# A four-layer sequence model on one core: the end of a channel mix beside the next layer norm, and key products whose sums grow in PSUM

## The chip, the cores and the metric

One NeuronCore of a Trainium2 chip runs the whole kernel in one launch. The metric is the device time of that launch in microseconds (us). TensorE (PE) does the matrix products; VectorE (DVE), ScalarE (ACT) and GpSimd (POOL) do the rest; the DMAs stand in the queue of SyncE (SP), which issues them in order.

## The reference

The input x is 8 sequences of 112 tokens with 512 channels, and there is a context of 8 x 375 x 512; everything is float32. Four layers follow each other: a small cross attention, two RWKV layers (time mix, then channel mix), and a last layer of two cross attentions with 16 heads of 128 channels and an MLP. What the change touches is the end of the second channel mix and the last layer:

```python
rr = jax.nn.sigmoid(xr2 @ fWr.T)
kk = jnp.square(jax.nn.relu(xk2 @ fWk.T))
x = x1 + rr * (kk @ fWv.T)
...
h = layer_norm(x, ln1_scale, ln1_offset)
q, k, v = h @ wq + bq, ctx @ wk + bk, ctx @ wv + bv
k, v = concat([k, bias_k]), concat([v, bias_v])
x = x + softmax(q @ k.T / sqrt(128)) @ v @ wo + bo
# the same with ln2, wq2, ..., then the MLP
x = x + gelu(layer_norm(x) @ w_fc1 + b_fc1) @ w_fc2 + b_fc2
```

## The kernel before, in words

Activations lie with their channels on the 128 partitions, in four chunks (NC = 4), and the 896 tokens in the free dimension, in two halves of 448 (NH). x stays in SBUF for the whole kernel. A projection (`project`, L152) makes, for each half h and output chunk o, one PSUM bank from four matmuls and gives it to an evacuation function.

**The order of the work.** The program is written as one stream for all engines. A framework keeps the engines' instructions in an order that it derives from that stream and from estimated costs (only the time mix, L632, has its order fixed by hand), and puts in the waits. Tiles come from pools; a tile of a pool with a few buffers waits until the last reader of the tile in the same buffer is done, and a pool that is opened after another was closed reuses its memory, so its tiles wait for the old ones there. `fill(n)` pulls n pieces of work from a generator named `filler`, which puts independent matmuls at that place of the stream: while the RWKV layers run it is `values()`, which makes the values of both cross attentions (and a few keys) ahead of time and stores them in DRAM; before each attention it is `first_keys()`.

**The second channel mix** (`channel_mix`, L674) norms x, mixes, and does three projections fk, fr, fv. fv's evacuation (`add`) multiplies the bank by rr on DVE (L722) and adds it to x on POOL (L723).

**The layer norm** (`layer_norm_half`, L165) works on one half of the tokens at a time: DVE sums the four channel chunks (L174, L176), one matmul with a matrix of 1/512 makes the mean for every channel (L178), DVE subtracts (L183), ACT squares (L185), DVE and PE make the variance in the same way, ACT takes the root (L190, Sqrt needs a table load), DVE the reciprocal (L191) and the product (L192), and ACT multiplies with the scale and adds the offset of each chunk (L194). Between the steps, `fill` puts matmuls.

**A cross attention** (`attention`, L1050; twice, i = 1, 2) norms x into h_in, and works in four groups gr of four heads. For each group it makes queries of all tokens, then goes through the eight sequences b: scores (L1167), softmax (L205 to L212), four transposes of the probabilities (L1170), their copies (L1174, L1176), the product with the values (L1180), the sum with a bias (L1187). Keys are made for two sequences b, b + 1 at a time. After a group comes its part of the output projection, which adds to x.

**Seven products instead of eight.** Queries, keys, output projections and MLP use a scheme of the Strassen kind: `seven` (L970) has a matrix product cut into 2 x 2 blocks made from seven block products, of sums of blocks of the weight (`weight_sums`, four POOL instructions, L957 to L960) and sums of blocks of the other operand (`token_sums`, four DVE instructions, L965 to L968; for keys the sums of the context lie in DRAM, and are loaded as four tiles cs of 375 KB, beside cx and cy, the plain context, by `key_pieces`, L1060). A block product is two matmul calls of the program, and shows as four instructions on PE. It is done for two halves m of the output chunks, so a pair of sequences and a group take 14 block products. In `seven`, each m uses the banks of the tag mm, of which there are two: the first product is copied out as p1 by ACT (L1001); the sums u2 = p + p1 (L1011) and u3 = p + u2 (L1016) are made by DVE as it reads the banks, and DVE adds them again to the later banks as it writes the keys (L1088); one product per m goes straight to the keys by an ACT copy (L1086). That is 4 ACT copies and 10 DVE additions from PSUM for a pair.

**Around the norms.** `attention` opens with `filler = first_keys()`, which loads the group's key weight, makes its POOL sums and yields the 14 products of the first pair; fill(3), then the norm with fills of 2, 2, 4 and 2, 2, 2, then the token sums, the queries and the loop over the sequences, which takes what is left of the filler. POOL also copies one column of bias into each key tile (L1160).

**The pools of layer 3** (`layer3`) are opened in this order: t3v (key sums with two buffers, the cs tiles, u2 and u3), t3k (cx, cy, three key tiles, values), t3 (h_in, q, t_h and others), t3w, and the PSUM pools.

Of the kernel before, what the change touches and what calls it, by code (L numbers as in the profile page):

```python
# [22 lines left out]
F32 = mybir.dt.float32  # L23
# [6 lines left out]
P = 128  # L30
B, L, C, S = 8, 112, 512, 375
N = B * L
# [9 lines left out]
HG = 4  # L42
# [66 lines left out]
def tile_kernel(ctx: ExitStack, tc: tile.TileContext, d: dict, out: bass.AP):  # L109
# [39 lines left out]
    def mm(ps, name):  # L149
        return ps.tile([P, 512], F32, tag="mm", name=name)  # L150

    def project(ps, w, rhs, evacuate, name, hs=(0, 1)):  # L152

        for h in hs:
            for o in range(NC):
                p = mm(ps, f"ps_{name}_{o}_{h}")[:, :NH]
                for k in range(NC):
                    nc.tensor.matmul(
                        p, w[:, k, o * P : (o + 1) * P], rhs(k, h), start=k == 0, stop=k == NC - 1
                    )  # L160
                evacuate(o, h, p)

    def layer_norm_half(ps, work, y, h, scale, offset, name, room=None, bank=None, fills=(2, 2, 4)):

        def small(tag, what):
            if room is not None:
                return room[1][:, h, int(tag == "rstd")]
            return work.tile([P, NH], F32, tag="rstd", name=f"{tag}_{what}_{name}_{h}")  # L170

        def over_channels(z, what):
            part = small("part", what)
            nc.vector.tensor_add(part, z[:, 0], z[:, 1])  # L174
            for c in range(2, NC):
                nc.vector.tensor_add(part, part, z[:, c])  # L176
            p = bank(f"{what}_{name}_{h}") if bank else mm(ps, f"{what}_{name}_{h}")[:, :NH]
            nc.tensor.matmul(p, mean_c, part, start=True, stop=True)  # L178
            return p

        mean = over_channels(halves(x, h), "mean")
        fill(fills[0])
        nc.vector.tensor_sub(y, halves(x, h), mean.unsqueeze(1).to_broadcast([P, NC, NH]))  # L183
        sq = work.tile([P, NC, NH], F32, tag="half", name=f"sq_{name}_{h}") if room is None else room[0][h]
        nc.scalar.activation(sq, y, AF.Square)  # L185
        fill(fills[1])
        var = over_channels(sq, "var")
        fill(fills[2])
        rstd = small("rstd", "")
        nc.scalar.activation(rstd, var, AF.Sqrt, bias=eps)  # L190
        nc.vector.reciprocal(rstd, rstd)  # L191
        nc.vector.tensor_mul(y, y, rstd.unsqueeze(1).to_broadcast([P, NC, NH]))  # L192
        for c in range(NC):
            nc.scalar.activation(  # L194
                y[:, c, :], y[:, c, :], AF.Identity, bias=column(offset, c), scale=column(scale, c)
            )

    def layer_norm(ps, work, dst, scale, offset, name, room=None, bank=None):
# [473 lines left out]
            project(ps, w_o, lambda c, h: halves(y[:, c, :], h), add, f"o{n}")  # L672

    def channel_mix(n, pre, names, first):  # L674
        with (
            tc.tile_pool(name=f"c{n}", bufs=1) as one,
            tc.tile_pool(name=f"cw{n}", bufs=2) as work,
# [44 lines left out]
                nc.vector.tensor_mul(y, p, y)  # L722
                nc.gpsimd.tensor_add(xs, xs, y)  # L723

            project(ps, f_v, lambda c, h: halves(kk[:, c, :], h), add, f"fv{n}")

    def rwkv_layers():
        with tc.tile_pool(name="rc", bufs=1) as one:
# [219 lines left out]
    def weight_sums(pool, tag, w, u):  # L948


        if tag == "wv":
            y = pool.tile([P, NC, C], F32, tag=tag, name=f"ws{u}")
            y = [y[:, j].rearrange("p (k o) -> p k o", k=2) for j in range(4)]
        else:
            y = [pool.tile([P, 2, 256], F32, tag=f"{tag}{j}", name=f"ws{j}{u}", bufs=1) for j in range(4)]
        a11, a12, a21, a22 = (w[:, k : k + 2, o : o + 256] for o in (0, 256) for k in (0, 2))
        nc.gpsimd.tensor_add(y[0], a21, a22)  # L957
        nc.gpsimd.tensor_sub(y[1], y[0], a11)
        nc.gpsimd.tensor_sub(y[2], a11, a21)
        nc.gpsimd.tensor_sub(y[3], a12, y[1])  # L960
        return y
# [8 lines left out]
    def seven(ps, work, w, s, b, t, n, put, u):  # L970
# [35 lines left out]
        for m in range(2):  # L1006
# [18 lines left out]
            yield  # L1025
            put(1, m, q, u2)

    def quarters(y):

        return [halves(y[:, k : k + 2], h) for h in range(2) for k in (0, 2)]  # L1030
# [16 lines left out]

        return put

    def attention(i, h_in, work, kv, ps, ps2, keep, mlp_norm):  # L1050
        nonlocal filler
        pre = "L3_xattn_"
        scale = 1.0 / math.sqrt(HD)
# [6 lines left out]
        def key_pieces(gr, b, w, kts):  # L1060


            u = f"{i}_{gr}_{b}"
            if ("wk", i, gr, b) in shared:
                for j in range(2):
                    kts.append(kv.tile([P, HG, T], F32, tag="kt", name=f"k{u}_{j}", bufs=3))
                    for t in range(3):
                        y = shared["wk", i, gr, b + j][:, t]
                        nc.sync.dma_start(kts[-1][:, :, t * CT : (t + 1) * CT], y)
                return  # L1070
            cx = kv.tile([P, NC, S], F32, tag="cx", name=f"cx{u}", bufs=2)
            nc.sync.dma_start(cx, d["ctxT"][:, b])
            t = [shared["pool"].tile([P, 3, 2, CT], F32, tag="cs", name=f"cs{u}_{j}", bufs=4) for j in range(4)]
            for y, pos in zip(t, (BLOCKS + 1, 2, 4, 6)):
                at = (3 * (b // 2) * BLOCKS + pos) * BLOCK
                from_ = shared["blocks"][:, at : at + 3 * BLOCKS * BLOCK].rearrange("p (c n) -> p c n", c=3)
                nc.sync.dma_start(y.rearrange("p c k s -> p c (k s)"), from_[:, :, :BLOCK])
            b22 = kv.tile([P, 2, S], F32, tag="cx2", name=f"cy{u}", bufs=1)
            nc.sync.dma_start(b22, d["ctxT"][:, b + 1, 2:])
            kt = [kv.tile([P, HG, T], F32, tag="kt", name=f"k{u}_{j}", bufs=3) for j in range(2)]  # L1080
            kts += kt

            def put(j, o, p, y):
                dst = kt[j][:, o, :S]
                if y is None:
                    nc.scalar.copy(dst, p)  # L1086
                else:
                    nc.vector.tensor_add(dst, p, y)  # L1088

            t = [y.rearrange("p c k s -> p k c s") for y in t]  # L1090
            yield from seven(ps, work, *w, (cx[:, :2], cx[:, 2:], b22), t, S, put, f"k{u}")

        kts, w_ks = [], []

        def first_keys():
            w_ks.append(key_weight(0))
            yield from key_pieces(0, 0, w_ks[0], kts)

        def ln_bank(name):
            return ps2.tile([P, HG, L], F32, tag="av", name=name).rearrange("p a b -> p (a b)")  # L1100


        scaled = keep.tile([P, 2 * NC + HEADS], F32, tag="scaled", name=f"scaled{i}")
        for at, n, v in ((0, NC, f"ln{i}_scale"), (NC, NC, f"ln{i}_offset"), (2 * NC, HEADS, f"bq{i}")):
            nc.scalar.mul(scaled[:, at : at + n], vecs[:, _COL[pre + v] : _COL[pre + v] + n], scale)
        over = keep.tile([P, HEADS], F32, tag="over", name=f"over_k{i}")
        bias_k, bk = (vecs[:, _COL[pre + v] : _COL[pre + v] + HEADS] for v in (f"bias_k{i}", f"bk{i}"))
        nc.vector.tensor_sub(over, bias_k, bk)
        filler = first_keys()
        room = keep.tile([P, NC, N], F32, tag="q", name=f"room{i}")  # L1110
        t_h = keep.tile([P, 3, 2, NH], F32, tag="t_h", name=f"t_h{i}")
        fill(3)
        layer_norm(ps, work, h_in, scaled[:, :NC], scaled[:, NC : 2 * NC], f"ln3_{i}", ([halves(room, h) for h in range(2)], t_h), ln_bank)
        token_sums(nc.vector, *quarters(h_in), t_h)

        rows = kv.tile([HEADS, HD], F32, tag="rows", name=f"bvr{i}", bufs=1)
# [5 lines left out]
        def queries(gr):  # L1122

            w = weight(f"{pre}wq{i}", gr)
            q = keep.tile([P, HG, N], F32, tag="q", name=f"q{i}_{gr}")

            def put_q(h, o, p, y):
                bias, dst = column(scaled, 2 * NC + gr * HG + o), halves(q[:, o, :], h)
# [13 lines left out]
        for gr in range(NG):  # L1142
# [6 lines left out]
            for b in range(B):  # L1149
                u = f"{i}_{gr}_{b}"  # L1150
                tok = slice(b * L, (b + 1) * L)
                if b % 2 == 0:
                    if gr and not b:
                        w_ks.append(key_weight(gr))
                    for _ in filler if gr == b == 0 else key_pieces(gr, b, w_ks[gr], kts):
                        pass
                    if not b and not ends:
                        s_o = weight_sums(keep, "ws", w_o, f"o{i}_{gr}")
                kt = kts.pop(0)
# [54 lines left out]
                for _ in out_pieces:  # L1214
                    pass

    def mlp(h_in, work, ps, keep, t_h):
        pre = "L3_xattn_"


        def hidden(gr):


            w = weight(f"{pre}w_fc1", gr)
            hid = keep.tile([P, NC, N], F32, tag="q" if gr % 2 else "ctxt", name=f"hid_{gr}")

            def put(h, o, p, y):
                bias, dst = vec(f"{pre}b_fc1", gr * NC + o), halves(hid[:, o, :], h)
# [42 lines left out]

    def layer3():
        with (
            tc.tile_pool(name="t3v", bufs=2) as shared["pool"],
            tc.tile_pool(name="t3k", bufs=2) as kv,
            tc.tile_pool(name="t3", bufs=1) as keep,
            tc.tile_pool(name="t3w", bufs=2) as work,
            tc.tile_pool(name="t3p", bufs=2, space=PSUM) as ps,
        ):
            h_in = keep.tile([P, NC, N], F32, name="h_in")  # L1280
            with tc.tile_pool(name="t3s", bufs=1, space=PSUM) as ps2:
                def mlp_norm(h, bank):
                    if not h:
                        room = keep.tile([P, 3, 2, NH], F32, tag="t_h", name="t_mlp")
                        shared["t_mlp"] = room
                        squares = halves(h_in, 1)
                    else:
                        squares = halves(keep.tile([P, NC, N], F32, tag="q", name="room_mlp"), 1)
                    pre = "L3_xattn_ln_mlp_"
                    room = [None, squares] if h else [squares, None]  # L1290
                    room = room, shared["t_mlp"]
# [2 lines left out]
                    )  # L1294

                for i in (1, 2):
                    attention(i, h_in, work, kv, ps, ps2, keep, mlp_norm)
            mlp(h_in, work, ps, keep, shared["t_mlp"])

    shared["spill"] = ctx.enter_context(tc.tile_pool(name="spill", bufs=1, space=bass.MemoryType.DRAM))  # L1300
    shared["blocks"] = shared["spill"].tile([P, (UNITS + 3) * BLOCKS * BLOCK], F32, name="blocks")
# [83 lines left out]
```

## Time and profile before

| what | value |
|---|---|
| median of 3 runs | 3063.15 us (3061.47 to 3063.49) |
| the profiled execution | 3068.96 us |
| its span, from the first instruction to the last | 3067.1 us |
| PE busy | 2936.8 us, 96% |
| DVE, ACT, POOL busy | 55%, 27%, 25% |
| mean granted clock of PE | 0.978 |
| DMA | 401.59 MB, 131 GB/s on average |

Durations in the text are from the profiled execution; instants are microseconds from the start of its span. The last projection of the second channel mix runs from about 1506 to 1530, the first attention from there to about 2188, the second from there to about 2850, and the MLP to the end. In a row of the profile, `a<-b,c` means that the instruction writes a and reads b and c, by the names of the tiles in the program; x before a number is the count; a bracket at the end gives the idle time of the engine before the instruction and what it is thought to have waited for. "PE" rows are matmuls, "PEld" rows their weight loads, which overlap.

### The profile page before, as it was taken

Reading aid. Unit: us, or ns where it says so; the run is one execution under the profiler, and the core shown is the slowest. Engines: PE = TensorE matmul, PEld = TensorE weight load, DVE = VectorE, ACT = ScalarE, POOL = GpSimd, SP = SyncE. Lnnn points to the kernel's source line nnn. Section 1 sums busy time; section 2 is a strip of 40 time slices with the busy share of each in tenths; the row PEclk is TensorE's granted clock in tenths of the full one; section 3 lists DMA queues with packets and bytes.
Section 4 is the critical chain, followed back from the end, with each engine's and each line's share of the span. In section 5 each row is a group of like instructions: output and inputs, shape, how many; then the busy total and the mean of one; then the engine's idle time right before and its main releaser. Section 6 shows DMA issues by size and latency. Waiting matters only on the chain.

```text
span 3067.1 us, 29702 instructions
## 1 busy us (share of the span) xinstructions
PE 2936.8 (96%) x10130; PEld 1585.1 (52%) x10130; DVE 1698.1 (55%) x2556; ACT 834.5 (27%) x1730; POOL 767.3 (25%) x668
## 2 busy tenths in 40 slices
PE   8989999998999999989989999999999999999999
PEld 4734433333434433337446666656566665656544
DVE  1433279876133289865165555655756454645555
ACT  2122145442232144532132222212222121212311
POOL 2232246642232257542210202020001101010030
PEclk9989999999999999999989999999999999999999
DMA  7322288963112299854234353424333343423110
GB/s 253 131 76 71 74 237 250 272 185 110 66 54 70 79 267 266 259 151 146 71 99 147 112 158 102 151 84 142 108 100 115 119 146 100 146 92 101 48 55 24
DMA packets 192054, 401.59 MB, mean 131 GB/s; under 512 B 26856, under 2 KB 112392, under 8 KB 185120
## 3 DMA queue, kind: packets, MB, share of 16 engines
q1 hardware_dynamic: 191904, 399.70, 42.0%
q8 instruction: 81, 1.33, 0.2%
q14 instruction: 69, 0.57, 0.1%
HBM read 321.85 MB, written 77.91 MB: 130 GB/s over the span
## 4 chain that ended last, share of the span: by engine, by line
PE 49%; DVE 2%; ACT 1%; issue 0%; POOL 0%; ACTq 0%; DVEq 0%; POOLq 0%
PE av L1180 6%; PE sc L1167 5%; PE ps_k1k L983 5%; PE ps_k7k L983 5%; PE ps_k5k L983 5%; PE pt L1170 3%; PE ps_k6k L983 2%; PE ps_k7q L983 2%; PE ps_k5q L983 2%; PE ps_k1q L983 1%; PE ps_k5o L983 1%; PE ps_k7o L983 1%; PE ps_k5fc L983 1%; PE ps_k7fc L983 1%; PE ps_k1o L983 1%; PE ps_k6q L983 1%
## 5 line engine op out<-in xcount | busy, mean ns | idle before, releaser
L839 PE MATMUL ps_vk<-wv,cv 128*128 128x512 f32 x1336 | 619.2, 611 | 52.4 <-DVE k L864 15.6
L839 PEld LDWEIGHTS ps_vk<-wv,cv 128*128 128x128 f32 x1336 | 251.5, 194 | 401.1 <-issue 303.0
L210 ACT ACTIVATE prob<-sc,top 112x376 f32<-112x376 f32 (+1 forms) x264 | 151.8, 575 | 709.6 <-DVE top L207 588.3
L649 POOL TENSOR_TENSOR rs<-st,r 128x896 f32<-128x896 f32 x128 | 246.7, 1928 | 226.7 <-DVE st L645 189.9
L645 DVE TENSOR_TENSOR_SCAN st<-decay,kv 128x904 f32<-128x904 f32 x128 | 260.4, 2035 | 15.6 <-DMA cv<-blocks 3.4
L1167 PE MATMUL sc<-k,q 128*112 128x376 f32 x512 | 200.6, 484 | 1.0 <-ACT prob L210 0.8
L1180 PEld LDWEIGHTS av<-pts,v 125*128 125x128 f32 (+1 forms) x1536 | 183.2, 191 | 30.0 <-DVE pts L1176 15.1
L1180 PE MATMUL av<-pts,v 125*128 125x112 f32 (+1 forms) x1536 | 186.6, 275 | 1.0 <-DVE pts L1176 1.0
L1160 POOL COPY k<-over_k 128x4 f32<-128x4 f32 x64 | 15.8, 253 | 678.3 <-PE sc L1167 610.0
L983 PE MATMUL ps_k1k<-cx,w_L_xattn_wk 128*128 128x375 f32 x480 | 177.1, 481 | 2.3 <-ACT rstdk L1001 2.3
L207 DVE TENSOR_REDUCE top<-sc 112x1 f32<-112x376 f32 (+1 forms) x264 | 143.6, 545 | 29.3 <-PE sc L1167 14.7
L641 DVE TENSOR_TENSOR kv<-vp,k 128x904 f32<-128x904 f32 x128 | 140.9, 1101 | 32.0 <-ACT vp L543 26.1
L922 ACT COPY k<-ps_vk 128x512 f32<-128x512 f32 (+1 forms) x153 | 89.0, 582 | 170.8 <-PE ps_vk L839 161.3
L1170 PEld LDWEIGHTS pt<-ident,prob 112*125 112x125 f32 (+1 forms) x768 | 97.6, 175 | 61.5 <-DVE prob L212 36.0
L212 DVE TENSOR_SCALAR prob<-prob,total 112x376 f32<-112x376 f32 (+1 forms) x264 | 120.7, 460 | 7.1
L983 PEld LDWEIGHTS ps_k1k<-cx,w_L_xattn_wk 128*128 128x128 f32 x480 | 89.3, 191 | 60.1 <-issue 3.2
L1170 PE MATMUL pt<-ident,prob 112*125 112x112 f32 (+1 forms) x768 | 116.3, 273 | 2.9 <-DVE prob L212 2.8
L543 ACT COPY vp<-vj 128x896 f32<-128x896 f32 x124 | 112.8, 910 | 11.6 <-DMA vj<-rows 7.6
L1187 DVE TENSOR_TENSOR ctxt<-av,bv 128x448 f32<-128x448 f32 x64 | 40.0, 624 | 126.6 <-PE av L1180 126.6
L933 POOL TENSOR_TENSOR k<-k,k 128x512 f32<-128x512 f32 (+1 forms) x51 | 67.4, 1322 | 133.6 <-ACT k L932 110.2
L1167 PEld LDWEIGHTS sc<-k,q 128*112 128x112 f32 x512 | 78.8, 176 | 41.1 <-ACT prob L210 6.1
L983 PE MATMUL ps_k7k<-cs,wsk 128*128 128x375 f32 x240 | 88.5, 480 | 0.6 <-DVE k L1088 0.6
(372 smaller groups left out, 4719.6 us busy)
## 6 DMA issues: line engine op xcount, KB each, us to landing
vj<-rows SPq DMA_DIRECT2D x124, 448.0 KB
cv<-blocks SPq DMA_DIRECT2D x181, 251.5 KB
cs<-blocks SPq DMA_DIRECT2D x120, 375.0 KB
wvs<-k SPq DMA_DIRECT2D x128, 256.0 KB
v<-wvs SPq DMA_DIRECT2D x64, 512.0 KB
cx<-in_ctxT SPq DMA_DIRECT2D x38, 750.0 KB
v<-wvs SPq DMA_DIRECT2D x64, 252.0 KB
wvs<-k SPq DMA_DIRECT2D x64, 224.0 KB
```

The lines of the kernel that those rows point to most:

```text
L207: nc.vector.tensor_reduce(top, scores, AX.X, ALU.max, negate=True)
L210: nc.scalar.activation(prob, scores, AF.Exp, bias=top, accum_out=total)
L212: nc.vector.tensor_scalar(prob, prob, total, None, ALU.mult)
L543: nc.scalar.copy(vp[:, :, 1:], by_batch(vjs.pop((c, j))))
L641: nc.vector.tensor_mul(flat(kv), flat(vp), flat(k[:, c]))
L645: nc.vector.tensor_tensor_scan(flat(st), flat(decay[:, c]), flat(kv), 0.0, ALU.mult, ALU.add)
L649: nc.gpsimd.tensor_mul(by_batch(rs), st[:, :, :L], by_batch(r[:, c, :]))
L839: nc.tensor.matmul(to, left, right, start=start and n == 0, stop=k == 1, skip_group_check=True)
L983: nc.tensor.matmul(to, lhsT, rhs, start=start and k == 0, stop=k == 1, skip_group_check=not start)
L1167: nc.tensor.matmul(sc, q[:, o, tok], kt[:, o, :], start=True, stop=True)
L1170: nc.tensor.transpose(pt[t][:nt, o, :], prob[:, t0 : t0 + nt], ident[:L, :L])
L1180: nc.tensor.matmul(av[:, o, :], v[:nt, t, o * HD : (o + 1) * HD], pts[:nt, t, o, :], start=t == 0, stop=t == 2,)
```

## The change

It has five parts.

1. The fv projection of the second channel mix is cut into pieces (`values_pieces`). The first half of the tokens is done as before. The second half becomes the filler of the norm of the first half: that half's norm of layer 3 is computed inside `channel_mix`, into two tiles of the weights' pool (y and sq), without the scale; one piece is pulled ahead of it and one at each of its three fill places. `attention` later applies scale and offset from y into h_in (`scale_by_channel`).
2. A new pool, near, is opened ahead of the other pools of layer 3, and so lies where the pool of the values was. It holds h_in, q (and the norm's room), t_h, scaled, over and the context tiles cx.
3. `first_keys` makes the keys of two pairs (sequences 0, 1 and 2, 3) instead of one. The fills around the norms become 2 and 3, 3, 4 for each half, with fill(8) after them; the loop over the sequences stops pulling once the pair that it needs is made.
4. The keys use `chained` in place of `seven`: the same block products with the same operands in another order, in two banks per m. One bank grows through four of them (k1, then + k6, then + k7, and at the end + t3's), and is copied out after each; the other takes the rest. So u2 and u3 are copies of a bank that grows on. For a pair this makes 10 ACT copies, 4 DVE additions that read PSUM and 2 DVE additions in SBUF; in the first group's first two pairs ("busy") it makes 14 ACT copies and 6 POOL additions in SBUF.
5. The POOL sums of a key weight have one buffer instead of two; the key tiles have four instead of three.

Cut to its core:

```diff
+            def values_pieces(h):
+                for o in range(NC):
+                    project(ps, f_v, lambda c, h: halves(kk[:, c, :], h), add, f"fv{n}", [h], [o])
+                    yield
...
+                for _ in values_pieces(0):
+                    pass
+                filler = values_pieces(1)
+                fill(1)
+                y, sq = (
+                    wpool.tile([P, NC, C], F32, tag="w", name=f"{what}_ln3")[:, :, :NH] for what in ("y", "sq")
+                )
+                layer_norm_half(ps, work, y, 0, None, None, "ln3_1", ([sq], None), None, (1, 1, 1))
+                for _ in filler:
+                    pass
+                shared["normed"] = y
...
+    def chained(ps, work, w, s, b, t, n, dst, u, busy):
...
+        for m in range(2):
+
+            one, two = (mm(ps, f"ps_{what}{u}_{m}")[:, :n] for what in (("k1", "k5") if m == 0 else ("k5", "k1")))
+            grows, other = (one, two) if m == 0 else (two, one)
+            p1, u2, u3 = (tile_of(what, m) for what in ("p1", "u2", "u3"))
+            for p, left, right, start, to, add in (
+                (grows, lambda k: w[:, k], b11, True, p1, None),
+                (other, lambda k: s()[0][:, k], t[0], True, dst(1, 2 + m), None),
+                (grows, lambda k: s()[1][:, k], t[1], False, u2, None),
+                (other, lambda k: s()[3][:, k], b22, False, dst(1, m), u2),
+                (grows, lambda k: s()[2][:, k], t[2], False, u3, None),
+                (other, lambda k: w[:, 2 + k], b21, True, dst(0, m), p1),
+                (grows, lambda k: w[:, 2 + k, 256:], t[3], False, dst(0, 2 + m), None),
+            ):
...
+                yield
+                if add is None or busy:
+                    nc.scalar.copy(to, p)
+                    if add is not None:
+                        nc.gpsimd.tensor_add(to, to, add)
+                else:
+                    nc.vector.tensor_add(to, p, add)
+                if to is u3:
+                    (nc.gpsimd if busy else nc.vector).tensor_add(dst(1, 2 + m), dst(1, 2 + m), u3)
...
-            yield from seven(ps, work, *w, (cx[:, :2], cx[:, 2:], b22), t, S, put, f"k{u}")
+            yield from chained(
+                ps, work, *w, (cx[:, :2], cx[:, 2:], b22), t, S, lambda j, o: kt[j][:, o, :S], f"k{u}", gr == 0 and b < BH
+            )
...
         def first_keys():
+
             w_ks.append(key_weight(0))
-            yield from key_pieces(0, 0, w_ks[0], kts)
+            for b in (0, 2):
+                yield from key_pieces(0, b, w_ks[0], kts)
+                made.append(b)
...
-        fill(3)
-        layer_norm(ps, work, h_in, scaled[:, :NC], scaled[:, NC : 2 * NC], f"ln3_{i}", ([halves(room, h) for h in range(2)], t_h), ln_bank)
+        room = [halves(room, h) for h in range(2)], t_h
+        scales = scaled[:, :NC], scaled[:, NC : 2 * NC]
+        for h in range(2):
+            if i == 1 and not h:
+                scale_by_channel(halves(h_in, 0), shared.pop("normed"), *scales)
+            else:
+                fill(2)
+                layer_norm_half(ps, work, halves(h_in, h), h, *scales, f"ln3_{i}", room, ln_bank, (3, 3, 4))
+        fill(8)
...
         with (
+            tc.tile_pool(name="t3n", bufs=1) as near,
             tc.tile_pool(name="t3v", bufs=2) as shared["pool"],
```

## The prediction

> **What bounds the kernel now.** I read the page first (busy shares, then the chain that ended last), then the busy time by stretch, then PE's waits, then the timelines around the two holes.
>
> ```profile
> PE 2936.8 (96%) x10130; PEld 1585.1 (52%) x10130; DVE 1698.1 (55%) x2556; ACT 834.5 (27%) x1730; POOL 767.3 (25%) x668
> ```
>
> TensorE is busy for 2936.8 of 3067.1 us, so only idle PE time and PE time at a low clock can be won; the change removes no matmul. The busy time by stretch (PE's comes first, the granted clock after POOL's) shows where both are:
>
> ```profile
> 1480.00:1530.00 50.00, 50.00 (x134) 25.07 (x132) 5.26 (x9) 6.17 (x10) 7.95 (x7) 1.00 0.12 42
> 1530.00:1597.00 67.00, 50.79 (x134) 25.95 (x134) 43.20 (x51) 18.19 (x29) 13.27 (x12) 0.87 0.33 101
> 2100.00:2190.00 90.00, 88.43 (x393) 57.52 (x392) 57.45 (x128) 18.38 (x50) 6.51 (x8) 1.00 0.41 132
> 2190.00:2260.00 70.00, 62.14 (x204) 34.92 (x203) 45.76 (x69) 23.98 (x44) 5.92 (x8) 0.93 0.23 71
> ```
>
> The stretches before each norm of layer 3 are full; the two that hold the norms lose 16.2 and 7.9 us, and their clock falls to 0.87 and 0.93. PE's waits there:
>
> ```profile
> PE mean_ln L178 <- POOL k L1160: 9.2, 1, 9.2
> PE ps_k6q L983 <- DVE t_h L966: 8.7, 2, 5.1
> ```
>
> The first is named after a POOL copy that nobody needs; the timelines (start, duration, work) show the real one, DVE's sums over channels:
>
> ```profile
> 1505.92 24.22 PE L158 MATMUL ps_fv<-kk,w_L_xattn_Wfv_None 128*128 128x448 f32 x64
> ...
> 1539.38 1.83 PE L178 MATMUL mean_ln<-t_h,mean_c 128*128 128x448 f32 x2 [9.24 <-POOL k L1160]
> ...
> 1578.01 3.35 PE L983 MATMUL ps_k6q<-t_h,ws1q 128*128 128x448 f32 x4 [3.53 <-DVE t_h L966]
> 1581.16 3.01 PE L983 MATMUL ps_k7q<-h_in,ws2q 128*128 128x448 f32 x4
> 1584.00 1.67 PE L983 MATMUL ps_k5q<-t_h,ws0q 128*128 128x448 f32 x4
> ```
> ```profile
> 1532.20 3.30 DVE L174 TENSOR_TENSOR t_h<-x 128x448 f32<-128x448 f32 x2
> 1535.42 4.35 DVE L176 TENSOR_TENSOR t_h<-t_h,x 128x448 f32<-128x448 f32 x4
> ...
> 1545.03 0.63 DVE L174 TENSOR_TENSOR t_h<-room 128x448 f32<-128x448 f32 x1 [1.76 <-ACT room L185]
> ```
> ```profile
> 1533.37 1.64 POOL L959 TENSOR_TENSOR ws2q<-w_L_xattn_wq 128x512 f32<-128x512 f32 x1
> ```
>
> So in transition 1 PE ends fv at 1530.1, waits 9.2 us for x, POOL's add and six channel sums, then later 3.5 us for the token sums (L965-968) before the query products. Transition 2 has only the second hole, with 5.1 us:
>
> ```profile
> 2227.24 3.32 PE L983 MATMUL ps_k6q<-t_h,ws1q 128*128 128x448 f32 x4 [5.12 <-DVE t_h L966]
> 2230.36 2.68 PE L983 MATMUL ps_k7q<-h_in,ws2q 128*128 128x448 f32 x4
> ```
>
> **What the Trainium skill says.** "TensorE: Matmul & The Clock Gate", What's actually happening: after an idle window of about 3.4 us PE runs at half rate until it has been busy about as long. The trace agrees: after idle 3.5 us a query product takes 3.35 and 3.01 us, then 1.67. "SBUF — State Buffer", Who interferes with whom: a DVE tensor_tensor with both inputs in SBUF contends with GpSimd for a shared port. It agrees: L174 takes 1.65 us beside POOL's weight sums, 0.63 alone, and the POOL sum 1.64 instead of 1.26. "PSUM — Partial Sum Buffer", Engine vs sequencer instructions: the ACT, DVE and POOL queues are strictly first in, first out, and matmuls keep program order; so I walk each queue in its order.
>
> **The change, part by part.** Elapsed and work up to the last query product, at the rates of full stretches:
> Transition 1, from the middle of fv (1518.0) to 1596.03: 78.1 us. Work: half of fv 12.0 (24.22/2), four norm matmuls 3.0 (0.75 each, from starts 1551.84 to 1552.59), 14 key products 17.7 (1.265 each), bv 0.2, 14 query products 21.0 (1.503 each, the start pitch), two scores 1.3: 55.2. Lost: 22.9 us.
> Transition 2, 2188.12 to 2244.89: 56.8 us, work without fv 43.2. Lost: 13.6. No more than 36 us can be won.
>
> (a) *fv beside the norm, first half made in spare weight tiles.* The last fv half (12 us of PE) now lies beside half 0's chain: channel sums, subtract 2.02, Square 1.70, sums, Sqrt 0.63 with its table load 1.28, reciprocal 2.94, multiply 2.01. Its x is complete at 1520.1 (POOL's fourth add of the half ends there). PE's order is fv 0, mean, fv 1, fv 2, variance, fv 3, a key product (1.27), mean of half 1. The variance is ready about 1.1 us late (queued behind it: fv 3 and all else), so fv ends near 1532.6. Half 1's sums stand on DVE behind the reciprocal and multiply of half 0, and run beside POOL: mean at 1538 to 1540. Of the 9.2 us hole I keep 4.5.
> Four scales per half (2.72 us for four) stay on ACT; half 0's now read y and write h_in.
>
> (b) *Tiles moved.* h_in and the queries' room lie where the values were; the cs tiles and the key sums come to lie over the channel mix's tiles. From the built order: on SP's queue the key weight now waits for fr's end (1506; it came at 1417), the query weight for half 0's squares (about 1529), and the four cs loads for POOL's last add (about 1535; issued at 1464 before), with cy, bvr, v and the next query weight behind them. A 1 MB weight took 4.1 us and the four cs loads 6 us together in the trace, so the first key product that reads cs can start at about 1537 to 1541.7. POOL makes the four key sums after its last add, 4 x 1.27 to 1.64 us = 5.1 to 6.6 (done by 1469 before): the first at 1536, the last at 1541. Those hide under the 4.5 us already counted, or add 2. Without that cover they would cost 5 to 6. The query sums follow on POOL, needed only near 1570. The key sums' single buffer holds back the next group's sums, 5 us of POOL, which lie beside the last two batches and the output projection (over 50 us): nothing.
>
> (c) *28 key products instead of 14.* 17.7 us more of filler. In transition 1 I find 6 of them (7.6 us) before the queries' end, in transition 2 all 14. They are moved, not new: each us of them in a hole comes off later.
>
> (d) *Growing sums.* PE work is the same. Evacuation per pair:
>
> ```profile
> L1086 ACT COPY k<-ps_k1k x60: 471/471/473, 1547.0 to 2837.8; 128x375 f32<-128x375 f32 x60
> L1088 DVE TENSOR_TENSOR k<-ps_k5k,u3k x60: 539/549/550, 1552.0 to 2851.8; 128x375 f32<-128x375 f32 x60
> ```
>
> Before: 4 ACT copies and 10 DVE adds. After, in 26 of 30 pairs: 10 copies and 6 adds (ACT +2.8 us, DVE -2.2); in the 4 beside norms: 14 copies and 6 POOL adds, DVE none, which frees 5.5 us of DVE per pair for the norm. A steady pair takes 31.05 us by the trace for 30.7 of PE work, so the 26 have at most 0.35 x 26 = 9 us to give. What the new ACT copies cost behind exponentials no row shows: bound +8 (0.3 us each pair), or -5; I take 0.
>
> Sum. Transition 1: left are 1.1 (variance), 4.5 (mean), 1.5 (slow clock after it), 2 (copies and loads), 2 (copies behind the second four scales, near 1558): 11.1; won 22.9 - 11.1 = 11.8, bounds 5 to 17. Transition 2: the keys begin at once and cover the sums; stalls 0.4 (mean), 0.7 (Square), 2.7 (two sets of scales), 0.7 (clock): 4.5; won 9.1, bounds 4 to 12. Together 20.9: the profiled execution (span 3067.1, 3068.96 with its ends) would give 3048.1. It stands 5.8 us above the median of the runs, 3063.15; the same gain there gives 3042.
>
> **The rivals.**
> *Late operands* (small gain): cs and key sums land together after 1541.5, so the fillers can't run while half 1's mean is awaited, and PE is left at half clock. Won only 5 + 4 = 9: 3054. For it: SP's and POOL's order above; against: a key product and fv itself need neither.
> *Evacuation becomes the bound* (slower): PE returns to a bank after one product, 1.265 us; a copy (0.47) behind two exponentials (0.575 each) comes at 1.62. With 0.36 us lost on 3 or 4 of 10 copies, a steady pair loses 1.2: 26 x 1.2 = 31, less 21: +10, 3073. It decides from 20.9/26 = 0.8 us a pair. For it: the copies stand in ACT's order between exponentials; against: ACT is 27% busy and DVE, which it relieves, 55%.
> *Nothing*: the keys moved early leave PE idle in the first softmaxes, and what was won in the holes is given back: 3061. Against: the key tiles have four buffers instead of three, so the next pair's products can follow.
> *More*: both transitions near their bounds, with steady pairs better by 3: -30, 3033.
>
> **How the numbers follow.** Forecast (3034 to 3051) 0.60, late operands 0.17, more 0.06, nothing 0.08, slower 0.09. A measurement of this kernel can tell 0.2% (6 us). Faster by more than that (below 3057): 0.60 + 0.06 + 0.16 = 0.82; within: 0.09; slower: 0.09. The likeliest is 3042. The range goes from all bounds good (17 + 12 + 5 = 34: 3029) to the weak end of late operands (3058); beyond it lie slower and most of nothing.
>
> **What would show it.** Right: no 9 us wait at a mean, fv's second half broken by norm matmuls, at most 5 us before half 1's mean; no 5 us hole ahead of k6q in either transition; a steady pair still near 31.0 us. Wrong: k5k waiting for cs or the key sums over 3 us; PE waiting on ACT copies of the keys by some tenths each pair; holes at the first softmaxes.

## The result and the profile after

| | before | after |
|---|---|---|
| median of 20 runs each | 3068.87 us (3057.52 to 3074.88) | 3066.89 us (3054.52 to 3078.93) |
| ratio, with its 95% interval | 1 | 0.9997 (0.9985 to 1.0008) |
| the profiled execution, span | 3067.1 us | 3056.5 us |

The change makes no difference that can be measured: a gain of 21 us was forecast, and about 1 us came, with an interval from 4.6 us faster to 2.5 us slower. (More runs of the kernel before were made for the comparison; their median lies 5.7 us above that of the first three.)

The two spans must not be compared as they stand. The order of the matmuls is the same up to the middle of fv in the second channel mix, and yet this point is reached at 1518.0 us before and at 1506.4 after. Those 11.6 us belong to the two executions: up to there PE's clock stood at half for 106 us in the one and for 68 us in the other. The profiles of the experiments below, whose matmuls have the same order up to this point, reach it between 1505.7 and 1522.6. From there to the start of the last matmul it is 1545.0 us before and 1545.9 after. So I compare stretches from one named matmul to another.

TensorE is as busy as before (the line of the page):

```profile
PE 2930.4 (96%) x10130; PEld 1574.3 (52%) x10130; DVE 1627.0 (53%) x2412; ACT 926.6 (30%) x1926; POOL 798.6 (26%) x692
```

DVE lost 71 us of work and ACT gained 92, from the growing sums. The busy time by stretch, with the two windows of each transition put back by what the kernel is ahead there (11.6 and 16.3 us; PE's busy time is the first figure after the comma, its clock stands behind POOL's):

```profile
1468.40:1518.40 50.00, 48.80 (x131) 24.41 (x130) 12.38 (x17) 9.16 (x12) 7.15 (x7) 1.00 0.07 21
1518.40:1585.40 67.00, 60.06 (x165) 31.66 (x164) 30.88 (x32) 23.25 (x42) 31.96 (x27) 0.92 0.44 144
2083.70:2173.70 90.00, 87.15 (x372) 55.11 (x371) 53.69 (x119) 23.53 (x62) 11.33 (x11) 1.00 0.41 131
2173.70:2243.70 70.00, 66.03 (x200) 36.20 (x199) 37.31 (x40) 30.25 (x56) 22.00 (x20) 1.00 0.32 99
```

PE does 60.1 and 66.0 us of work in the two norm stretches, where it did 50.8 and 62.1, and its clock is higher. The long waits are gone or halved; PE's waits, from 1400 to 2360:

```profile
PE mean_ln L179 <- DVE t_h L177: 4.1, 1, 4.1
PE ps_k5k L1081 <- ACT k L1084: 2.5, 3, 1.3
```

So the transitions did what was forecast, in kind. The next table shows where the gain went. Its stretches are (batches count from 0): transition 1 from the start of fv's second half to the first value product of batch 5 in the first group, where every kernel has made the same three pairs of keys; groups 1, the rest of the first attention up to batch 4 of its last group; transition 2 from there to batch 5 of the second attention's first group; groups 2 up to the last batch; the end from there to the last matmul.

| kernel (one profile each, us) | transition 1 | groups 1 | transition 2 | groups 2 | end (MLP) | ratio to before in the runs |
|---|---|---|---|---|---|---|
| before | 156.9 | 455.0 | 193.9 | 544.7 | 194.6 | 1 |
| after | 146.9 | 457.9 | 188.6 | 547.2 | 205.3 | 0.9997 (0.9985 to 1.0008) |

10.0 and 5.3 us are won in the transitions; 2.9 and 2.5 are lost in the groups and 10.7 in the MLP, which the change was not thought to touch. 5.1 us of the MLP's loss stand in PE's waits ahead of ps_k6fc (PE's waits from 2840 to the end, before and after). After the change two of the three are over 3 us long, where the longest before was 1.4:

```profile
PE ps_k6fc L983 <- DVE x L1046: 1.9, 3, 1.4
```
```profile
PE ps_k6fc L1008 <- DVE x L1110: 7.0, 3, 3.4
```

and the timelines of PE, DVE and POOL after show how one of them comes about:

```profile
2936.52 6.18 PE L1008 MATMUL ps_k1fc<-hid,w_L_xattn_w_fc 128*128 128x448 f32 x16
2946.05 1.83 PE L1008 MATMUL ps_k6fc<-t_hid,ws1fc 128*128 128x448 f32 x2 [3.35 <-DVE x L1110]
```
```profile
2938.08 2.13 DVE L990 TENSOR_TENSOR t_hid<-hid 128x896 f32<-128x896 f32 x1 [0.73 <-ACT hid L1302]
2940.25 2.05 DVE L991 TENSOR_TENSOR t_hid<-hid,t_hid 128x896 f32<-128x896 f32 x1
2942.22 2.15 DVE L992 TENSOR_TENSOR hid<-hid 128x896 f32<-128x896 f32 x1
2944.29 1.08 DVE L993 TENSOR_TENSOR t_hid<-hid,t_hid 128x896 f32<-128x896 f32 x1
2945.29 1.14 DVE L1110 TENSOR_TENSOR x<-ps_k1fc,x 128x448 f32<-128x448 f32 x2
```
```profile
2936.77 1.27 POOL L982 TENSOR_TENSOR wsfc<-w_L_xattn_w_fc 128x512 f32<-128x512 f32 x1 [13.70 <-PE ps_k5fc L1008]
2938.00 1.27 POOL L984 TENSOR_TENSOR wsfc<-w_L_xattn_w_fc 128x512 f32<-128x512 f32 x1
2939.23 2.12 POOL L983 TENSOR_TENSOR wsfc<-wsfc,w_L_xattn_w_fc 128x512 f32<-128x512 f32 x1
2941.42 1.99 POOL L985 TENSOR_TENSOR wsfc<-w_L_xattn_w_fc,wsfc 128x512 f32<-128x512 f32 x1
```

The sums of the next hidden group's weight (wsfc) use the buffer of the key sums, which the change made single. POOL must now wait for the last product that reads the old sums (ps_k5fc, at 2936.5), and then does its four sums just when DVE makes the four token sums of the hidden layer. Three of these take 2.1 us instead of 1.09, and PE's next products wait for them and for the addition to x behind them. It is the collision that the Trainium skill describes ("SBUF — State Buffer", Who interferes with whom) for a DVE instruction with two inputs in SBUF beside a GpSimd instruction that reads SBUF, and the trace agrees: 1.09 us alone, 2.13 beside POOL. The kernel before has a small form of it: ahead of its wait of 1.4 us, only the last of the four token sums meets POOL (2.16 us).

### The profile page after: what moved, and what is told of

Same layout as the page of the kernel before. It is cut to its first block, busy times and chain, and to the rows that moved or that the text cites. A ratio compares the mean times of both kernels' runs of the same rounds, so it can differ in the third digit from the quotient of the medians.

```text
span 3056.5 us, 29703 instructions
## 1 busy us (share of the span) xinstructions
PE 2930.4 (96%) x10130; PEld 1574.3 (52%) x10130; DVE 1627.0 (53%) x2412; ACT 926.6 (30%) x1926; POOL 798.6 (26%) x692
## 4 chain that ended last, share of the span: by engine, by line
PE 49%; DVE 2%; ACT 1%; issue 0%; DMA 0%; POOL 0%; POOLq 0%; ACTq 0%
PE ps_k1k L1081 9%; PE ps_k5k L1081 7%; PE av L1250 6%; PE sc L1237 5%; PE pt L1240 3%; PE ps_k1q L1008 2%; PE ps_k7q L1008 2%; PE ps_k5q L1008 2%; PE ps_k7fc L1008 1%; PE ps_k5fc L1008 1%; PE ps_k5o L1008 1%; PE ps_k7o L1008 1%; PE ps_k1o L1008 1%; PE ps_o L158 1%; PE ps_k6q L1008 1%; PE ps_fr L158 1%
## 5 line engine op out<-in xcount | busy, mean ns | idle before, releaser
L1250 PEld LDWEIGHTS av<-pts,v 125*128 125x128 f32 (+1 forms) x1536 | 185.7, 193 | 31.4 <-DVE pts L1246 16.2
L1081 PE MATMUL ps_k1k<-cs,wsk 128*128 128x375 f32 x480 | 178.7, 481 | 1.5 <-ACT p1k L1084 1.5
L1081 PEld LDWEIGHTS ps_k1k<-cs,wsk 128*128 128x128 f32 x480 | 89.4, 189 | 59.6 <-ACT p1k L1084 1.8
L1088 DVE TENSOR_TENSOR k<-ps_k5k,u2k 128x375 f32<-128x375 f32 x52 | 28.5, 547 | 159.5 <-PE ps_k5k L1081 158.2
```

Source lines behind the costliest of these rows:

```text
L1081: nc.tensor.matmul(y, lhsT, rhs, start=start and k == 0, stop=k == 1, skip_group_check=True)
L1250: nc.tensor.matmul(av[:, o, :], v[:nt, t, o * HD : (o + 1) * HD], pts[:nt, t, o, :], start=t == 0, stop=t == 2,)
```

## The experiments

All ratios are to the kernel before, with their 95% intervals.

**The MLP's sums apart.** Sums for hidden groups 2 and 3 go into key tiles, which nobody uses in the MLP:

```diff
+        elif tag == "kt":
+            y = [pool.tile([P, HG, T], F32, tag="kt", name=f"ws{j}{u}", bufs=4) for j in range(2)]
...
-            return hid, project7(ps, work, w, lambda: weight_sums(shared["pool"], "wv", w, u), h_in, t_h, put, u)
+            return hid, project7(ps, work, w, lambda: weight_sums(*((kv, "kt") if gr > 1 else (shared["pool"], "wv")), w, u), h_in, t_h, put, u)
```

> The changed kernel, with the MLP's weight sums for its second and third hidden group in two free key tiles each (tag kt) instead of the single buffer that they share with the first group's sums. Everything else is as in the changed kernel. Theory A (what the transitions won is given back in the MLP, because the sums of hidden group 2 and 3 must wait for the last product of the group before, and then run on POOL beside the token sums on DVE): the two waits of 3.5 us ahead of ps_k6fc fall to about 1, the stretch from the last batch's value product to the end falls from 205 to about 197 to 199, and the whole is 6 to 8 us (0.2 to 0.26%) below the kernel before. Theory B (the MLP's loss was only a low PE clock drawn in that one execution): the stretch varies with the granted clock between 195 and 205 whatever the buffers, and the ratio to the kernel before stays at 1.000.

Measured: 0.9974 (0.9963 to 0.9984), 8 us below before. The end stretch is 198.4 us, and the wait has its old size (PE's waits to the end, and the group of the first token sum):

```profile
PE ps_k6fc L1011 <- DVE x L1113: 1.9, 3, 1.4
```
```profile
L993 DVE TENSOR_TENSOR t_hid<-hid x4: 1093/1093/1093, 2909.0 to 3039.7; 128x896 f32<-128x896 f32 x4
```

**One buffer in the kernel before.** The converse, with the orders of PE, DVE and ACT unchanged:

```diff
-            y = pool.tile([P, NC, C], F32, tag=tag, name=f"ws{u}")
+            y = pool.tile([P, NC, C], F32, tag=tag, name=f"ws{u}", bufs=1)
```

> The kernel before with one buffer instead of two for the key sums' tag (wv), nothing else: the orders of PE, DVE and ACT stay the same, only POOL's sums move. Theory A: two waits ahead of ps_k6fc in the MLP of 3 to 4 us each appear (1.4 and less before), the stretch from the last batch's value product to the end grows from 194.6 to 199 to 203, the attentions keep their length within 1 us, and the ratio is 1.0015 to 1.003. Theory B: no change beyond 0.1%.

Measured: 1.0020 (1.0011 to 1.0028), 6 us slower; the end stretch 205.1 us. The same wait and the same slow sum appear as after the change:

```profile
PE ps_k6fc L983 <- DVE x L1046: 7.0, 3, 3.3
```
```profile
L965 DVE TENSOR_TENSOR t_hid<-hid x4: 1092/1610/2134, 2901.3 to 3038.8; 128x896 f32<-128x896 f32 x4
```

Both experiments agree with theory A and against B. Some of the 10.7 us is the clock all the same, and the traces part the two. From the MLP's first product to the last matmul it takes 178.7 us before, 185.3 after, 178.5 in mlp_sums_apart and 185.2 here; in all fourteen profiles it is 185.2 to 185.4 in the five kernels with the single buffer, and 178.5 to 179.6 in the nine others. So the buffer costs 6.6 us, and the runs give 6. It is not waiting alone: in each of the five, PE stands at half clock for 6.8 us in all around these waits, and in none of the nine before the last matmul. The other 4.1 us lie ahead of that, between the last batch's value product and the MLP's first product (15.9 us before, 20.0 after): a window of 10.2 us at half clock stands there in this profile, in that of the change and in mlp_sums_apart, and not in that of before, though PE's waits ahead of it (about 1 us each) differ by 0.3 us at most.

**Keys by seven again.**

```diff
-            yield from chained(ps, work, *w, (cx[:, :2], cx[:, 2:], b22), t, S, lambda ..., f"k{u}", gr == 0 and b < BH)
+            yield from seven(ps, work, *w, (cx[:, :2], cx[:, 2:], b22), t, S, put, f"k{u}")
```

> The changed kernel with the keys made by seven as before (4 ACT copies and 10 DVE additions from PSUM a pair) instead of chained; two pairs beside the norms, tiles and fv as in the change. Theory A (growing sums help beside the norms, where they free DVE, and cost about 1 us a group elsewhere because PE runs out of keys or waits on ACT): the groups 1 to 3 go back by 0.8 to 1 us each (149.6 to 148.8 for group 1), 5 us in all, but the two transitions lose 4 to 8 us more, since DVE again has 10 additions a pair between the norm's steps: ratio to before 0.999 to 1.001. Theory C (the ACT copies of chained are what gave the gain back): the kernel is 5 us or more faster than the changed one, ratio 0.998.

Measured: 1.0010 (1.0002 to 1.0018). Groups 1 and 2 go back to 455.2 and 543.7 us; transition 1 loses most of what it had won (155.6), transition 2 keeps it (188.1). Theory A holds for the groups and for transition 1; its loss in transition 2 did not come. Theory C falls.

**One pair beside the norms.**

```diff
-            for b in (0, 2):
+            for b in (0,):
```

> The changed kernel, but first_keys makes only the first pair's keys (14 products instead of 28) beside the norms; fills, order and tiles as in the change. Theory A (the extra products fill the token sums' hole ahead of the query products): a wait of 3 to 5 us ahead of ps_k6q comes back in both transitions, with a low clock after it; transition 1 loses 4 to 6 us of what it won and transition 2 nearly all of its 7: total 8 to 12 us above the changed kernel, ratio 1.003. Rival D (one pair moved early is only lent, and the first softmaxes pay it back): no difference.

Measured: 1.0020 (1.0011 to 1.0030). Transition 2 is 196.1, more than before: the second pair is worth 7.5 us there, as theory A has it. Transition 1 stays at 147.3, so the second pair is worth nothing there, against the expectation.

**fv not split.**

```diff
-            if n == 1:
+            if True:
                 project(ps, f_v, ...)
...
-            if i == 1 and not h:
+            if False:
```

> The changed kernel, but the second channel mix's fv is done whole as before, and the first half's norm of layer 3 stands in the attention with the others; everything else as in the change. Theory A (of the 10 us won in transition 1, laying fv's second half beside the norm is the larger part, since nothing else can cover x's way through POOL and the channel sums): the wait of about 9 us ahead of the first mean comes back, with a low clock after it, and transition 1 (second half of fv to the sixth batch's value product, 147.0 in the changed kernel, 156.9 before) is 153 to 158; the other stretches stay; ratio to before 1.002. Rival E (the 28 key products and the free DVE carry the gain): transition 1 stays below 150, because key products fill the wait.

Measured: 1.0002 (0.9994 to 1.0009), transition 1 146.7 us. Theory A fell: the split gives nothing. Rival E had the number but not the cause, since one_pair_first keeps transition 1 as short without the second pair. DVE's timeline shows what covers the wait:

```profile
1519.23 0.63 DVE L177 TENSOR_TENSOR t_h<-t_h,x 128x448 f32<-128x448 f32 x1 [1.25 <-POOL x L729]
1520.37 0.62 DVE L728 TENSOR_TENSOR rr<-ps_fv,rr 128x448 f32<-128x448 f32 x1 [0.51 <-PE ps_fv L158]
1522.24 0.63 DVE L177 TENSOR_TENSOR t_h<-t_h,x 128x448 f32<-128x448 f32 x1 [1.25 <-POOL x L729]
```

The norm's channel sums into t_h run between fv's evacuations, each as soon as x's chunk is there, without any split. Before, all six stood behind fv's end. This gave theory F: the wait came from the tiles' place in memory.

**Only growing sums**, in the kernel before: chained as in the change, with busy always False.

```diff
-            yield from seven(ps, work, *w, (cx[:, :2], cx[:, 2:], b22), t, S, put, f"k{u}")
+            yield from chained(ps, work, *w, (cx[:, :2], cx[:, 2:], b22), t, S, lambda ..., f"k{u}", False)
```

> The kernel before with chained in place of seven for all keys (10 ACT copies, 4 DVE additions from PSUM and 2 in SBUF a pair; never the form with POOL), nothing else. Theory A (growing sums cost about 1 us in each group through the copies on ACT and help only beside a norm): groups 1 to 3 of an attention become longer by 0.5 to 1.2 us each (group 1: 148.8 to 149.6; group 2: 166.5 to 167.5), the transitions change by less than 3 us, ratio 1.000 to 1.002. Theory C' (the extra microsecond in a group comes from four key tiles or the other tiles, not from the copies): the groups keep 148.8 and 166.5, ratio 1.000.

Measured: 1.0018 (1.0008 to 1.0028); groups 457.7 and 545.7 us, transitions 154.7 and 193.4. So chained costs by itself, as theory A has it. PE's listed waits do not hold this cost: in groups 1 they are 0.0 us before and 0.4 here, of 2.7 us more.

**Growing sums beside the norms alone**, with the MLP's sums apart.

```diff
+            if gr == 0 and b < BH:
+                yield from chained(..., True)
+            else:
+                yield from seven(ps, work, *w, (cx[:, :2], cx[:, 2:], b22), t, S, put, f"k{u}")
```

> The changed kernel with the MLP's sums apart (as in mlp_sums_apart) and chained only for the two pairs beside each norm (14 ACT copies, 6 POOL additions); all other pairs by seven. Theory A (the three effects add up): transition 1 at 147 and transition 2 at 188.5 as in the changed kernel, groups 1 to 3 at 148.9 and 166.5 as before, the MLP at 195 to 199: 4 to 5 us below mlp_sums_apart, 12 to 13 us below the kernel before, ratio 0.9955 to 0.9965. If the groups' extra microsecond has another cause, it equals mlp_sums_apart, 0.9974.

Measured: 0.9946 (0.9929 to 0.9963): 147.4, 455.1, 186.1, 543.5, 195.9. The effects add up: 16 us below the kernel before (12 to 13 were expected).

**Only the tiles moved**, in the kernel before: the pool near, and nothing else of the change.

```diff
+            tc.tile_pool(name="t3n", bufs=1) as near,
             tc.tile_pool(name="t3v", bufs=2) as shared["pool"],
...
-        t_h = keep.tile([P, 3, 2, NH], F32, tag="t_h", name=f"t_h{i}")
+        t_h = near.tile([P, 3, 2, NH], F32, tag="t_h", name=f"t_h{i}")
```

(and so for h_in, q, room, scaled, over, cx)

> The kernel before with one part of the change: the pool near, opened first, with h_in, q, t_h, scaled, over and cx (so these no longer lie over the second channel mix's tiles, but the cs tiles and the key sums now do). All else as before: seven, one pair, fv whole, two buffers for the sums, three key tiles. Theory F (formed after fv_not_split: the wait of 9.2 us ahead of the first mean came from t_h's place, whose memory the channel mix held until x's last addition; with t_h elsewhere the channel sums run beside fv by themselves): no wait over 2 us ahead of the first mean; instead cs lands late (a wait of some us ahead of the first product that reads it); transition 1, 156.9 before, becomes 149 to 155. Theory A' (the split is what moves the sums): the wait ahead of the mean stays at 8 to 9 us.

Measured: 0.9975 (0.9965 to 0.9986). Transition 1 is 147.5 us, which is 9.4 of the 10.0 us that the change gains there. PE's timeline has no wait at the mean, and a short one for cs:

```profile
1534.59 3.95 PE L983 MATMUL ps_k1k<-cx,w_L_xattn_wk 128*128 128x375 f32 x12
1538.38 0.91 PE L178 MATMUL mean_ln<-t_h,mean_c 128*128 128x448 f32 x2
1539.13 1.43 PE L983 MATMUL ps_k1k<-cx,w_L_xattn_wk 128*128 128x375 f32 x4
1542.51 1.50 PE L983 MATMUL ps_k6k<-cs,wsk 128*128 128x375 f32 x4 [1.95 <-DMA cs<-blocks]
```

Theory F holds against A'. With the places, the derived order changed too: three key products now stand ahead of the mean, where the kernel before had none. Which of the moved tiles it was, t_h or over (whose subtraction stands ahead of the sums on DVE), was not separated.

**The best without the split, and the cs tiles loaded early.** unsplit_best is growing_only_beside_norms with fv whole. The other two exchange the places of cx and cs tiles:

```diff
-            cx = near.tile([P, NC, S], F32, tag="cx", name=f"cx{u}", bufs=2)
+            cx = (kv if b % 4 else near).tile([P, NC, S], F32, tag="cx", name=f"cx{u}", bufs=1)
-            t = [shared["pool"].tile([P, 3, 2, CT], F32, tag="cs", ..., bufs=4) for j in range(4)]
+            t = [(near if j < 2 else shared["pool"]).tile([P, 3, 2, CT], F32, tag="cs", ..., bufs=2) for j in range(4)]
```

> As growing_only_beside_norms, with fv done whole and the first half's norm in the attention (as in fv_not_split). Theory F (splitting fv gives nothing once t_h is free): transition 1 is 146 to 148.5 as with the split, the others the same, ratio 0.9945 to 0.9955. Theory A' : transition 1 is 4 us longer than with the split.

> As unsplit_best, with two of the four cs tiles in near and one of the two cx tiles out of it (same memory): the first two cs loads no longer wait for x's last addition. Theory F (what is left in transition 1 is the late cs): the wait of 4.6 us ahead of ps_k5k falls to 1 to 2 us (then the key sums on POOL come last), no low clock follows it, and transition 1 falls from about 147 to 141 to 144: ratio 0.9925 to 0.9940. If the key sums on POOL are as late as cs: 145 to 147, no gain.

> As growing_only_beside_norms (fv split), with the same exchange of cs and cx tiles. Theory F: here cs costs only 0.9 us and the wait of 4.1 us ahead of the second half's mean stays, which comes from DVE's order; transition 1 falls by 1 us at most (146 to 147.5), ratio 0.9940 to 0.9950.

Measured: 0.9941 (0.9918 to 0.9963), 0.9937 (0.9916 to 0.9957) and 0.9930 (0.9912 to 0.9948), with transition 1 at 146.2, 147.4 and 146.5 us. Without the split nothing is lost. Loading cs early gains nothing, and theory F's 141 to 144 us did not come. In unsplit_cs_early the wait ahead of k5k falls as expected, from 4.8 us for cs to 1.8 for the key sums on POOL, but a new one stands ahead of the variance, and a window of 3.4 us at half clock follows:

```profile
PE var_ln L179 <- DVE t_h L177: 2.6, 1, 2.6
PE ps_k5k L1084 <- POOL wsk L985: 1.8, 1, 1.8
```

In split_cs_early the 4.1 us ahead of the second half's mean, which were expected to stay, are gone, and the key sums are late in their place:

```profile
PE ps_k5k L1084 <- POOL wsk L985: 5.2, 1, 5.2
```

The intervals of these three overlap with each other and with that of growing_only_beside_norms.

**Without growing sums and without the split.** unsplit_best, with seven everywhere.

> As unsplit_best, with all keys by seven, so without chained anywhere: left of the change are the moved tiles and the second pair beside the norms, and the MLP's sums stand apart. Theory G (with fv whole and t_h free, DVE has room for seven's additions; chained only repairs what the split loads on DVE, where keys_by_seven had 155.6 in transition 1): transition 1 is 146 to 149, transition 2 187 to 189, the rest as in unsplit_best: ratio 0.9945 to 0.9960. Theory H (chained is needed beside any norm): transition 1 is 152 or more, ratio 0.9965 or more.

Measured: 0.9958 (0.9941 to 0.9975): 144.7, 455.3, 188.1, 544.9, 196.9. Theory G holds: beside a whole fv, seven is as good as chained in transition 1. PE is idle for 7.5 us there, against 14.5 in keys_by_seven. In transition 2 chained is 2 us better (186.1).

| kernel (one profile each, us) | transition 1 | groups 1 | transition 2 | groups 2 | end (MLP) | ratio |
|---|---|---|---|---|---|---|
| tiles_moved_only | 147.5 | 455.4 | 192.6 | 543.5 | 196.2 | 0.9975 |
| only_growing_sums | 154.7 | 457.7 | 193.4 | 545.7 | 195.3 | 1.0018 |
| before_one_buffer | 155.6 | 456.0 | 191.9 | 544.1 | 205.1 | 1.0020 |
| keys_by_seven | 155.6 | 455.2 | 188.1 | 543.7 | 202.9 | 1.0010 |
| one_pair_first | 147.3 | 459.5 | 196.1 | 546.6 | 202.7 | 1.0020 |
| fv_not_split | 146.7 | 457.4 | 188.6 | 547.0 | 205.2 | 1.0002 |
| mlp_sums_apart | 146.3 | 459.0 | 188.7 | 546.8 | 198.4 | 0.9974 |
| growing_only_beside_norms | 147.4 | 455.1 | 186.1 | 543.5 | 195.9 | 0.9946 |
| unsplit_best | 146.2 | 456.1 | 186.1 | 544.4 | 195.9 | 0.9941 |
| unsplit_cs_early | 147.4 | 455.0 | 186.1 | 543.7 | 196.3 | 0.9937 |
| split_cs_early | 146.5 | 455.0 | 186.1 | 544.4 | 195.8 | 0.9930 |
| unsplit_seven | 144.7 | 455.3 | 188.1 | 544.9 | 196.9 | 0.9958 |

The last five rows rest on 6 runs each, the others on 16 to 22.

## Why the prediction was wrong

**The step that failed** is in (b): "The key sums' single buffer holds back the next group's sums, 5 us of POOL, which lie beside the last two batches and the output projection (over 50 us): nothing." For the attention that was right: with the single buffer alone, groups 1 and 2 take 456.0 and 544.1 us, for 455.0 and 544.7 before. But the tag wv also holds the sums of the MLP's hidden groups, and there the sums are released at the very moment when DVE makes token sums on PE's path. Measured alone it costs 6 us (before_one_buffer); with the MLP's sums apart the changed kernel gains 7 us (0.9997 to 0.9974, mlp_sums_apart). I had looked at whether POOL's 5 us are hidden in the attention, and neither at the other stage that uses the tag nor at what POOL's work does to its neighbour on DVE. Nearly all the signs that the prediction named for being right came: no wait over 4.1 us at a mean, fv broken by the norm's matmuls, no hole ahead of k6q. None of them looked at the MLP.

**Growing sums, (d), "I take 0".** They cost 2.9 and 2.5 us in the groups of the two attentions: 5.4 us over the 22 pairs that lie there, 0.2 us a pair, and 0.18% when alone. The bound of +8 held this, the value taken did not. The rival that makes evacuation the bound had the direction, but put 1.2 us on a pair. That chained causes it is shown by keys_by_seven and only_growing_sums. Whether it is the ACT copies, the order of the products or the banks is not shown: PE's listed waits hold at most 0.4 us of it in groups 1, and the rest is spread thin over key, score and transpose products.

**fv beside the norm, (a).** The walk through the queues came true (PE's order, 1.2 us of waiting at the variance for 1.1, 4.1 at the second half's mean for 4.5), and the size was near (10.0 us won in transition 1 for 11.8), but the cause was wrong, so the near size is luck. I put the 9.2 us down to x's way through POOL and DVE after fv. The sums could have run beside fv all along; they waited for the memory of the channel mix. Moving the tiles, in which (b) saw only a cost, gives 9.4 us alone: PE's idle time in transition 1 falls from 16.2 us to 8.9, and the whole change leaves 8.1. The split then loads DVE so that seven no longer fits beside it (keys_by_seven 155.6, unsplit_seven 144.7), and chained repairs that. Two of the change's parts cancel each other here.

**Late operands.** As forecast, cs and the key sums are a little late: 0.9 us of waiting for cs with the split, 4.6 without it (fv_not_split), and with cs early the key sums on POOL hold up PE in its place (1.8 us without the split, 5.2 with it).

**The second pair, (c).** In transition 1, seven more products lie ahead of the queries (six were forecast), but they are worth nothing in the end (one_pair_first). In transition 2 they carry the gain: 5.3 us for 9.1 forecast, and 7.8 once seven makes the other pairs (growing_only_beside_norms).

**The sum.** Forecast -20.9; measured by stretches -10.0 - 5.3 + 2.9 + 2.5 + 10.7 = +0.8 us in the two profiles, of which 4.1 us of the last term are clock; the runs give -0.03%. The rival "Nothing" had the number, but not for its reason: from the last query product to the end of each transition PE has no listed wait, before or after.

## What to carry to other kernels

When a buffer is taken from a tag, follow the tag through the whole program: every tile that uses it can get a new wait, also far from the change, and the wait decides when that engine runs, and so beside whom. Before work is split to cover a wait, ask whether the waiting instruction's output tile is free; here a different place in memory did what the split was made for. And measure the parts of a combined change one by one: two of the five (moved tiles, a second pair) carry the gain, two (the single buffer, growing sums away from the norms) give it back, and one (the split) does nothing.

## What was not expected of the hardware

The spread of the runs goes with the granted clock: among the 20 runs of the changed kernel the spans reach from 3052.7 us at a mean clock of 0.985 to 3077.1 at 0.977. The spans differ by 0.8%, span times clock by 0.36%.

The Trainium skill ("TensorE: Matmul & The Clock Gate", What's actually happening) has the half rate begin after an idle window of about 3.4 us. The traces agree at the long waits (before: idle 3.5 us ahead of k6q, half clock for 6.8 us around its end), but not at the end of the last attention. No wait of PE there is longer than 1.3 us, and yet a window at half clock opens in most profiles: 10.2 us in the changed kernel, 3.4 in growing_only_beside_norms, none in the kernel before, beside waits of the same size. From the last batch's value product to the MLP's first product the fourteen profiles take 15.8 to 15.9 us without a window, 17.4 to 17.5 with one of 3.4 us, and 19.9 to 20.0 with one of 10.2. What decides which of them comes stays open.
